# Where six layer-norm tiles are transposed inside the first cross-attention of a fused six-stage kernel

## The chip, the cores and the metric

The kernel runs on one core of a Trainium2 chip. A core has a matrix engine (TensorE, PE in the profile; its weight loads are PEld), a vector engine (DVE), a scalar engine (ACT), GpSimd (POOL), and a queue that issues transfers (SP). Each engine works through its own instructions in order, and waits on semaphores for the others. [...] The metric is the device time of one execution in microseconds. Three runs of the kernel before gave 1981.14, 1982.46 and 1980.77 us, a median of 1981.14 us.

## The reference

The whole is two layers of a Perceiver: cross-attention, a Mamba-like mixer, a routed feed-forward, a second cross-attention, causal self-attention, and a quantized feed-forward, each on the layer norm of a residual stream `x` of 16 x 64 tokens by 512. The change lies in the first cross-attention, and in the layer norm that the second step needs:

```python
def _layernorm(x, axis=-1, eps=1e-05):
    m = jnp.mean(x, axis=axis, keepdims=True)
    v = jnp.var(x, axis=axis, keepdims=True)
    return (x - m) / jnp.sqrt(v + eps)
...
    # first cross-attention: 16 heads of 32, 1601 context keys for each of 16 sequences
    qh = (q @ Wq + bq).reshape(B, LQ, HEADS, D_K).transpose(0, 2, 1, 3)
    kh = (k @ Wk + bk).reshape(B, LKV, HEADS, D_K).transpose(0, 2, 1, 3)
    vh = (v @ Wv + bv).reshape(B, LKV, HEADS, D_K).transpose(0, 2, 1, 3)
    scores = jnp.einsum('bhqd,bhkd->bhqk', qh, kh) * scale
    attn = jax.nn.softmax(scores, axis=-1)
    out = jnp.einsum('bhqk,bhkd->bhqd', attn, vh)
    concat = out.transpose(0, 2, 1, 3).reshape(B, LQ, D_MODEL)
    return concat @ Wo + bo
...
x = x + _L0_xattn_ref(_layernorm(x, axis=-1), ctx_512, ctx_512, ...)
x = x + _L0_attn_ref(_layernorm(x, axis=-1), ...)
```

## The kernel before

All is float32. The 1024 tokens are eight tiles ("groups", `g`) of 128 rows; a group holds two sequences of 64. The first cross-attention runs over 32 units `u` (a sequence and half of its heads: `u // 2` is the sequence) and a 33rd pass that finishes the last unit. Every instruction in this loop is pinned (`pin`) to the order in which the program writes it, on each engine, so there is no planner between the text and the queues. One pass of the loop holds work of three units at once:

- `next_k`: projections of the keys of unit `u`, eight of them (`k_proj`, line 221), each two pairs of matmuls into a PSUM tile of the pool `ps_mm`, which ACT copies out with the bias (line 231). `ps_mm` has two buffers, and the value projections and `project` use it too.
- `maxima(u - 1)` and `shift(u - 1)` (lines 323 and 331): four transposes, a reduction on DVE (line 329), four transposes that spread the maxima, and seven additions on DVE (line 342). Their PSUM tiles `mt` and `nb` share the pool `ps_mx`, tag `mx`, which has one buffer. `maxima` follows the first of the eight key projections, `shift` the second.
- `next_exps`: the exponentials of unit `u - 1` on ACT (line 350), between the later key projections and behind the first scores.
- `scores(u, 0)`, `scores(u, 1)`, `scores(u, 2)`: matmuls into two double banks `sc0` and `sc1`, emptied by ACT (`keep`, line 278) and compared by DVE (line 294). The third call has a rest of 65 keys, `scl`, of which one half goes into `ps_mx`.
- `attend(u - 1, 0)` behind `scores(u, 1)`, and `attend(u - 1, 1)` behind `scores(u, 2)`: matmuls of 32 columns, tile `av`.
- `project(g)` when a group's four units are done, at `u` = 5, 9, 13, 17, 21 and 25 for the groups 0 to 5: four more matmuls, the addition to `x`, and `ln_stats` on DVE.

As soon as a group's `x` is final, its layer norm can be made for the next step. `ln_scale` (line 119) takes the square root of the variances on ACT and the reciprocal on DVE. The square root is not in the table of functions that Exp uses, so the program loads a table ahead of it, and another ahead of the next Exp. `ln_norm` (line 123) scales a group on DVE, at the start of a pass. `ln_transpose` (line 130) transposes the 128 x 512 result in four matmuls into one PSUM tile, and ACT copies it into `xnT` (line 135). `xnT` is the same tensor as `qo`, the queries and outputs of the attention, whose columns of a finished group are free. `NORM0` says which pass makes which group. Behind `ln_norm`, POOL adds a bias row to the group's `x` for the next step (line 143); this is not pinned and goes to where its operand is ready.

The kernel before takes the square roots of the groups 0 to 3 in pass 17 and of 4 and 5 in pass 25, and norms the groups in the passes 18, 19, 20, 21, 27 and 28. In each of these, the transposes stand between the third and the fourth key projection (lines 518 to 521) and use a buffer of `ps_mm`.

Of the kernel before, what the change touches and what calls it, by code (L numbers as in the profile page):

```python
# [9 lines left out]
F32 = mybir.dt.float32  # L10
# [5 lines left out]
P = 128  # L16
# [11 lines left out]
LN_EPS = 1e-5  # L28
NEG = -1.0e30

NORM0 = {18: (0,), 19: (1,), 20: (2,), 21: (3,), 27: (4,), 28: (5,)}
NPREP = 30
RND = 12582912.0
QMAX = 32767.0
# [8 lines left out]
def nkeys(c):  # L43
    return min(P, LK - c * P)
# [3 lines left out]
def perceiver_kernel(ctx: ExitStack, tc: tile.TileContext, x_d, ctxT_d, ctx_d, cols_d, rows_d,  # L48
# [5 lines left out]
    def pool(stack, name, bufs=1, side="left", **kw):  # L54
        return stack.enter_context(
            tc.tile_pool(name=name, bufs=bufs, side=side, reuse_waits="tile", **kw))
# [44 lines left out]
    def row(at, n=D):  # L101
        return rows[:, at:at + n]
# [16 lines left out]
    def ln_scale(g0, g1, pin=free):  # L119
        pin(s.activation(rstd[:, g0:g1], mv[:, g0:g1, 1], AF.Sqrt, bias=eps))  # L120
        pin(v.reciprocal(rstd[:, g0:g1], rstd[:, g0:g1]))
# [5 lines left out]
                            ALU.subtract, ALU.mult))  # L127
        return xn

    def ln_transpose(g, xn, ps_pool, pin=free, dst=None):  # L130
        ps = ps_pool.tile([P, 4, P], F32, name="ps", tag="mm")
        for c in range(4):
            pin(pe.transpose(ps[:, c, :], xn[:, c * P:(c + 1) * P], ident))  # L133
        dst = xnT if dst is None else dst
        pin(s.copy(dst[:, :, g * P:(g + 1) * P], ps))
# [58 lines left out]
    with ExitStack() as st1:  # L194
# [18 lines left out]
        ps_mm = pool(st1, "ps_mm", bufs=2, space=PSUM)  # L213
        pin = tc.keep_in_program_order

        def pmm(out, lhsT, rhs, start=True, stop=True):
            pin(pe.matmul(out, lhsT=lhsT, rhs=rhs, start=start, stop=stop))  # L217
# [33 lines left out]
        def scores(u, g):  # L251

            ks = range(4 * g, 4 * g + 4)
            last = KC - 1
            if g == 0:
                sts[u] = stp.tile([P, KC, 512], F32, name="st", tag="st")
            st = sts[u]
            sc = [ps_sc.tile([P, 4, 2 * P], F32, name="sc", tag=f"sc{r}") for r in range(2)]  # L260

            def one_chunk(out, k):
                n = nkeys(k)
                for i in range(2):
                    for r in range(2):
                        rows_ = slice(64 * r, 64 * r + 64)
                        pmm(out[r][:n, i * P:(i + 1) * P],
                            kts[u, i][rows_, k * P:k * P + n], qds[u % 2][rows_, i, :])

            for k in ks:  # L270
                one_chunk([sc[r][:, k - ks[0], :] for r in range(2)], k)
            if last == ks[-1] + 1:
                tail = [ps_mx.tile([P, 2 * P], F32, name="scl", tag="mx"),
                        ps_mm.tile([P, 2 * P], F32, name="scl", tag="mm")]
                one_chunk(tail, last)

            def keep(r):
                pin(s.copy(st[:, ks[0]:ks[-1] + 1, r * 256:(r + 1) * 256], sc[r]))  # L278

            if g == 0:  # L280
                keep(0)
                keep(1)
                first[u] = sc
                return

            keep(1)
            if last == ks[-1] + 1:
                n = nkeys(last)
                for r in range(2):
                    pin(s.copy(st[:n, last, r * 256:(r + 1) * 256], tail[r][:n]))  # L290
            for r in range(2):
                rm = rms[u][:, :, r * 256:(r + 1) * 256]
                for z in (0, 2):
                    pin(v.tensor_tensor(rm, rm, sc[r][:, z:z + 2, :], ALU.max))  # L294
                if r == 0:
                    keep(0)
# [48 lines left out]
        def exps(u, k):  # L345

            n = min(2, KC - k)
            m = nkeys(k + n - 1)
            f = flat(u)
            pin(s.activation(f[:m, k:k + n, :], f[:m, k:k + n, :], AF.Exp))  # L350
            if u == 2 * B - 1:
                return
            if k == 2:
                accs[u] = mxp.tile([P, 2, 512], F32, name="acc", tag="acc")
                pin(gp.tensor_tensor(accs[u], f[:, 0:2, :], f[:, 2:4, :], ALU.add))  # L355
            elif 2 < k and n == 2:
                pin(gp.tensor_tensor(accs[u], accs[u], f[:, k:k + 2, :], ALU.add))  # L357
            elif n == 1:
                pin(gp.tensor_tensor(accs[u][:m, 0], accs[u][:m, 0], f[:m, k, :], ALU.add))
# [72 lines left out]
        with ExitStack() as stq:  # L432
# [8 lines left out]
            for h in range(2):  # L441
                for e in range(4):
                    ps = psq.tile([P, 512], F32, name="ps", tag="mm")
# [24 lines left out]
        ps_mx = pool(st1, "ps_mx", space=PSUM)  # L468

        for u in range(U + 1):  # L470
            old, new = u >= 1, u < U
            k_at = iter(range(0, KC, 2))

            def next_exps(n):
                for _ in range(n if old else 0):
                    exps(u - 1, next(k_at))

            def next_k(i, z):
                if old and new:
                    k_proj(u, i, z)  # L480

            def next_v(*ks):
                for k in ks:
                    v_proj(u, k)

            if 0 < u <= NPREP:
                piece_load(u - 1, prep)
            if new:
                diagonal(u)
            if u < G:  # L490
                pin(gp.tensor_tensor(x[:, u, :], x[:, u, :], row(R_BO0), ALU.add))

            normed = [(g, ln_norm(g, pin)) for g in NORM0.get(u, ())]
            next_k(0, 0)
            if old and new:
                maxima(u - 1)
            next_k(0, 1)
            if not new:


                project(G - 2, lambda: maxima(u - 1), lambda: shift(u - 1))
                divide(u - 2)
                for k in range(0, KC, 2):
                    exps(u - 1, k)
                    for z in range(k, min(k + 2, KC)):
                        attend_chunk(u - 1, z)
                b, hf = (u - 1) // 2, (u - 1) % 2
                rs = mxp.tile([P, 2, LQ], F32, name="rs", tag="rs")
                pin(v.reciprocal(rs, avs[u - 1][2]))
                for i in range(2):  # L510
                    pin(v.tensor_tensor(qo[:, 2 * hf + i, b * LQ:(b + 1) * LQ], avs[u - 1][i],
                                        rs[:, i], ALU.mult))
                break
            if old:
                shift(u - 1)
            if u >= 2:
                divide(u - 2)
            next_k(0, 2)
            for g, xn in normed:
                ln_transpose(g, xn, ps_mm, pin)  # L520
            next_k(0, 3)
            for z in range(4):
                next_k(1, z)
                next_exps((1, 1, 0, 2)[z])
            if 1 < u <= NPREP + 1:
                piece_turn(u - 2, room[:, u % 2, :], pin)
            next_v(0, 1)
            scores(u, 0)
            next_exps(3)
            next_v(2)  # L530
            first_max(u, 0)
            next_v(3)
            first_max(u, 1)
            next_v(4, 5)
            if 0 < u <= NPREP:
                piece_scale(u - 1, pin)
            g = (u - 2) // 4
            if u >= 2 and (u - 2) % 4 == 3 and g < G - 2:
                project(g)
                ln_stats(g, pin)  # L540
                if g in (3, 5):
                    ln_scale(0 if g == 3 else 4, g + 1, pin)
            scores(u, 1)
            if old:
                attend(u - 1, 0)
            next_v(6, 7, 8, 9)
            if old:
                acc = accs[u - 1]
                pin(v.tensor_tensor(acc[:, 0], acc[:, 0], acc[:, 1], ALU.add))
            if 0 < u <= NPREP:  # L550
                piece_steps(u - 1, pin)
            scores(u, 2)
            if old:
                attend(u - 1, 1)
                sum_up(u - 1, accs[u - 1][:, 0])
            if 0 < u <= NPREP:
                piece_round(u - 1, pin)
            next_v(10, 11)
            last_max(u)
            next_v(12)  # L560
            if u % 2 and u // 2 + 2 < B:
                load_ctx(u // 2 + 2)
# [28 lines left out]
    with ExitStack() as st2:  # L591
# [141 lines left out]
        mt, xn = None, None  # L733
        for g in range(G):
# [7 lines left out]
            if g >= 2:  # L742
                ln_scale(g - 2, g - 1, pin)
                xn = ln_norm(g - 2)
# [31 lines left out]
    with ExitStack() as st3:  # L776
# [132 lines left out]
        for q in range(2):  # L909
            t = slice(q * 512, (q + 1) * 512)  # L910
            for i in range(NBLK):
                ps = ps3.tile([P, 512], F32, name="ps", tag="mm")
# [65 lines left out]
    with ExitStack() as st4:  # L978
# [18 lines left out]
        ps_mm = pool(st4, "ps_mm4", bufs=3, space=PSUM)  # L997
# [120 lines left out]
    mx = const.tile([P, 5, 24], F32, name="mx", tag="mx")  # L1118
# [132 lines left out]
    with ExitStack() as st6:  # L1251
# [30 lines left out]
        with ExitStack() as sta:  # L1282
# [57 lines left out]
            for f in range(FC):  # L1340
# [5 lines left out]
                for h in range(2):  # L1346
                    t = slice(h * 512, (h + 1) * 512)
                    ps = ps6.tile([P, 512], F32, name="ps", tag="mm")
# [118 lines left out]
```

## Time and profile before

| | |
|---|---|
| three runs, median (us) | 1981.14 |
| the profiled execution, its own time (us) | 1979.56 |
| its span, from the first to the last instruction (us) | 1977.8 |
| granted TensorE clock | 0.993 |
| ACT line 120, square root | 20 times, 294 / 296 / 302 ns |
| ACT line 120, table loads ahead of it | 13 times, 1283 ns each |
| ACT line 135, copy of a transposed group into `xnT` | 40 times, 576 / 586 / 726 ns |
| DVE line 126, scaling of a group | 46 times, 513 / 544 / 723 ns |

The three figures are the least, the median and the most. A busy PE says that matmuls were in flight; since they overlap, the time of a group of matmuls is best read from the start of its first to the start of what follows. Windows of a pass, below, are cut at the start of the reduction on line 329, which occurs once in each pass from 1 to 32.

### The profile page before, as it was taken

How to read it: one execution, taken by the hardware profiler on the slowest of the kernel's cores; microseconds unless marked ns; L12 is line 12 of the kernel's file. 1: busy time of each engine (PE TensorE's matmuls, PEld its weight loads, DVE VectorE, ACT ScalarE, POOL GpSimd, SP SyncE). 2: the span in 40 equal slices, each digit the busy share in tenths (PEclk: the TensorE clock that was granted, in tenths of full speed). 3: DMA queues.
4: the chain of work that ended last, by engine and by line, in shares of the span. 5: the costliest groups of instructions: out<-in, count | busy, mean ns of one | idle time of the engine just before them, and what ended most of it. 6: DMA issues, size and time to landing. Idle time of an engine off the chain costs nothing.

```text
span 1977.8 us, 38953 instructions
## 1 busy us (share of the span) xinstructions
PE 1925.4 (97%) x17069; PEld 1214.5 (61%) x17069; DVE 1167.2 (59%) x1934; ACT 812.5 (41%) x1137; POOL 621.3 (31%) x464
## 2 busy tenths in 40 slices
PE   8999999999999999999999999999999999999599
PEld 4677777677777777777777754445444554444234
DVE  3577777777777777777777765722203334329651
ACT  2445454455545454454545556310202232316700
POOL 1245555454545445464554522211002000000100
PEclk9999999999999999999999999999999999999899
DMA  6012011111211110121110030530155981001001
GB/s 216 1 46 56 14 55 46 45 23 45 56 46 23 46 50 18 46 56 36 32 46 18 29 135 23 172 96 1 53 213 200 407 335 64 0 19 45 0 0 43
DMA packets 110075, 141.14 MB, mean 71 GB/s; under 512 B 79520, under 2 KB 82096, under 8 KB 106320
## 3 DMA queue, kind: packets, MB, share of 16 engines
q1 hardware_dynamic: 109904, 138.64, 21.0%
q8 instruction: 134, 2.20, 0.5%
q14 instruction: 37, 0.30, 0.0%
HBM read 127.02 MB, written 11.60 MB: 70 GB/s over the span
## 4 chain that ended last, share of the span: by engine, by line
PE 93%; DVE 2%; issue 2%; ACT 2%; DMA 1%; POOL 0%; POOLq 0%; SPq 0%; ACTq 0%; DVEq 0%
PE ps L217 39%; PE ps L59 24%; PE sc L217 12%; PE av L217 6%; PE po L59 4%; PE u L217 2%; PE ps L133 1%; PE pbc L59 1%; PE mt L327 1%; PE nb L336 1%; PE scl L217 1%; PE pd L59 1%; POOL gate L1344 0%; DVE st L342 0%; PE pg L59 0%
## 5 line engine op out<-in xcount | busy, mean ns | idle before, releaser
L217 PE MATMUL ps<-wkv,ctxT 128*128 128x256 f32 (+1 forms) x1664 | 393.6, 387 | 1.8 <-DVE vt L242 1.6
L217 PE MATMUL ps<-ctxT,wkv 128*128 128x400 f32 (+1 forms) x1024 | 365.2, 503 | 11.5 <-DMA ctxT<-in_ctxT_dram 7.3
L217 PEld LDWEIGHTS ps<-wkv,ctxT 128*128 128x128 f32 (+1 forms) x1664 | 295.5, 185 | 75.4 <-ACT kt L231 13.8
L278 ACT COPY st<-sc 128x1024 f32<-128x1024 f32 x192 | 191.9, 1016 | 294.2 <-PE sc L217 281.5
L357 POOL TENSOR_TENSOR acc<-acc,st 128x1024 f32<-128x1024 f32 x124 | 293.4, 2366 | 22.6 <-ACT st L350 17.5
L242 DVE TENSOR_TENSOR vt<-ps,rows 128x256 f32<-128x256 f32 (+1 forms) x416 | 174.8, 421 | 176.8 <-PE ps L217 176.7
L217 PEld LDWEIGHTS ps<-ctxT,wkv 128*128 128x128 f32 x1024 | 189.1, 190 | 140.4 <-ACT kt L231 10.1
L231 ACT ACTIVATE kt<-ps,cols 128x400 f32<-128x400 f32 (+1 forms) x256 | 152.3, 595 | 270.5 <-PE ps L217 270.5
L342 DVE TENSOR_TENSOR st<-st,nb 128x1024 f32<-128x1024 f32 (+1 forms) x224 | 239.0, 1138 | 34.5 <-PE nb L336 34.5
L350 ACT ACTIVATE st<-st 128x1024 f32<-128x1024 f32 (+1 forms) x224 | 212.1, 993 | 7.2 <-DVE st L342 6.9
L217 PEld LDWEIGHTS sc<-qd,kt 64*128 64x128 f32 x3072 | 178.9, 188 | 34.4 <-issue 24.4
L217 PE MATMUL sc<-qd,kt 64*128 64x128 f32 x3072 | 197.3, 278 | 0.0
L294 DVE TENSOR_TENSOR rm<-rm,sc 128x512 f32<-128x512 f32 x256 | 169.2, 681 | 40.0 <-PE sc L217 35.6
L355 POOL TENSOR_TENSOR acc<-st 128x1024 f32<-128x1024 f32 x31 | 73.2, 2362 | 319.3 <-issue 174.7
L59 PE MATMUL ps<-xnT,w 128*128 128x512 f32 x256 | 112.7, 594 | 0.0
L59 PE MATMUL ps<-w,hT 128*128 128x512 f32 x256 | 110.2, 592 | 0.0
L217 PE MATMUL av<-st,vt 128*32 128x64 f32 x6656 | 108.5, 220 | 0.9 <-ACT st L350 0.7
L217 PEld LDWEIGHTS av<-st,vt 128*32 128x32 f32 x6656 | 97.2, 110 | 11.8 <-issue 5.3
L180 POOL TENSOR_TENSOR w<-w,wsc 128x512 f32<-128x512 f32 x36 | 38.5, 1068 | 196.8 <-DVE w L179 196.8
L1344 POOL TENSOR_TENSOR gate<-up,gate 128x1024 f32<-128x1024 f32 x5 | 11.8, 2357 | 249.1 <-ACT up L1343 249.1
L59 PEld LDWEIGHTS ps<-w,hT 128*128 128x128 f32 x256 | 48.6, 190 | 61.2 <-issue 61.2
L59 PE MATMUL ps<-xnT,wuT 128*128 128x512 f32 x192 | 82.8, 592 | 0.0
(246 smaller groups left out, 2197.5 us busy)
## 6 DMA issues: line engine op xcount, KB each, us to landing
cT<-in_ctxT_dram SPq DMA_DIRECT2D x16, 1601.0 KB, 9.7
cN<-in_ctx_dram SPq DMA_DIRECT2D x16, 1536.0 KB, 11.0
ctxT<-in_ctxT_dram SPq DMA_DIRECT2D x15, 1601.0 KB, 6.4
mk<-kept SPq DMA_DIRECT2D x16, 512.0 KB, 3.9
w<-in_w_dram SPq DMA_DIRECT2D x1, 4096.0 KB, 13.4
w<-in_w_dram SPq DMA_DIRECT2D x4, 1024.0 KB, 7.3
w<-in_wgate_dram SPq DMA_DIRECT2D x12, 256.0 KB, 2.8
wgt<-room SPq DMA_DIRECT2D x48, 64.0 KB, 2.0
```

The lines of the kernel that those rows point to most:

```text
L59: pe.matmul(out, lhsT=lhsT, rhs=rhs, start=start, stop=stop)
L133: pin(pe.transpose(ps[:, c, :], xn[:, c * P:(c + 1) * P], ident))
L180: pin(gp.tensor_tensor(w, w, sc.unsqueeze(2).to_broadcast([P, 16, 32]), ALU.mult))
L217: pin(pe.matmul(out, lhsT=lhsT, rhs=rhs, start=start, stop=stop))
L231: pin(s.activation(kts[u, i][:, o:o + n], ps[:, :n], AF.Identity, bias=col(C_BK0 + c)))
L242: pin(v.tensor_tensor(t[:n, :], ps[:n, :], row(R_BV0 + e, 256)[:n, :], ALU.add))
L278: pin(s.copy(st[:, ks[0]:ks[-1] + 1, r * 256:(r + 1) * 256], sc[r]))
L294: pin(v.tensor_tensor(rm, rm, sc[r][:, z:z + 2, :], ALU.max))
L342: pin(v.tensor_tensor(f[:m, k:k + n, :], f[:m, k:k + n, :], nb[:m].unsqueeze(1).to_broadcast([m, n, 512]), ALU.add))
L350: pin(s.activation(f[:m, k:k + n, :], f[:m, k:k + n, :], AF.Exp))
L355: pin(gp.tensor_tensor(accs[u], f[:, 0:2, :], f[:, 2:4, :], ALU.add))
L357: pin(gp.tensor_tensor(accs[u], accs[u], f[:, k:k + 2, :], ALU.add))
```

## The change

Three edits. `ln_transpose` gets the tag of its PSUM tile as an argument. In the loop of the first attention, the call moves from between the third and the fourth key projection to behind `scores(u, 1)`, ahead of `attend(u - 1, 0)`, and takes its tile from `ps_mx` and not from `ps_mm`. And the six groups are normed in the passes 26 to 31, with one `ln_scale` for all six in pass 25; that of pass 17 is gone. `ln_norm` stays at the start of its pass.

```diff
-NORM0 = {18: (0,), 19: (1,), 20: (2,), 21: (3,), 27: (4,), 28: (5,)}
+NORM0 = {26: (0,), 27: (1,), 28: (2,), 29: (3,), 30: (4,), 31: (5,)}
...
-    def ln_transpose(g, xn, ps_pool, pin=free, dst=None):
-        ps = ps_pool.tile([P, 4, P], F32, name="ps", tag="mm")
+    def ln_transpose(g, xn, ps_pool, pin=free, dst=None, tag="mm"):
+        ps = ps_pool.tile([P, 4, P], F32, name="ps", tag=tag)
...
             next_k(0, 2)
-            for g, xn in normed:
-                ln_transpose(g, xn, ps_mm, pin)
             next_k(0, 3)
...
                 ln_stats(g, pin)
-                if g in (3, 5):
-                    ln_scale(0 if g == 3 else 4, g + 1, pin)
+                if g == 5:
+                    ln_scale(0, g + 1, pin)
             scores(u, 1)
+            for g, xn in normed:
+                ln_transpose(g, xn, ps_mx, pin, tag="mx")
             if old:
                 attend(u - 1, 0)
```

Built, the changed kernel has on ACT one square root and two table loads fewer in this stage, on DVE one reciprocal fewer, and the same number of instructions on POOL and SP. The order on ACT in a normed pass is: the two `keep` copies of `scores(u, 1)`, the copy of line 135, then the first `keep` of `scores(u, 2)`. On PE the transposes stand right between the scores and `attend`, and the first of them carries no semaphore wait of its own. The scaling on DVE and POOL's addition of line 143 move with their passes. Behind the first attention, the order on all engines is as before.

## The prediction

> **What bounds the kernel now.** I read the engine totals and the chain of waits first, on the page:
>
> ```profile
> PE 1925.4 (97%) x17069; PEld 1214.5 (61%) x17069; DVE 1167.2 (59%) x1934; ACT 812.5 (41%) x1137; POOL 621.3 (31%) x464
> PE 93%; DVE 2%; issue 2%; ACT 2%; DMA 1%; POOL 0%; POOLq 0%; SPq 0%; ACTq 0%; DVEq 0%
> ```
>
> TensorE sets the end: 93% of the chain is its own matmuls. So an edit counts by what it adds to or takes from PE's sequence, and work of DVE, ACT and POOL counts only where PE waits for it. To see where PE waits, I cut the first attention into its passes. The columns are the stretch, its length, then busy time and instructions of PE, PEld, DVE, ACT and POOL, the granted clock and the DMA share; here are passes 17, 18, 19, 23, 25, 26 and 27:
>
> ```profile
> 621.25:658.07 36.82, 36.82 (x421) 26.51 (x420) 27.52 (x47) 18.74 (x26) 16.96 (x12) 1.00 0.10 18
> 658.07:693.53 35.46, 34.30 (x417) 25.40 (x416) 25.89 (x42) 19.02 (x26) 18.26 (x13) 1.00 0.20 60
> 693.53:727.82 34.29, 34.04 (x417) 25.57 (x416) 25.90 (x43) 17.64 (x25) 18.25 (x13) 1.00 0.10 20
> 833.21:866.54 33.33, 33.33 (x413) 25.14 (x412) 25.33 (x41) 17.16 (x24) 16.98 (x12) 1.00 0.11 21
> 899.88:936.70 36.82, 36.82 (x421) 26.52 (x420) 27.07 (x46) 18.73 (x26) 16.95 (x12) 1.00 0.10 19
> 936.70:971.21 34.51, 33.60 (x413) 24.98 (x412) 25.90 (x43) 18.55 (x25) 16.99 (x12) 1.00 0.20 61
> 971.21:1005.50 34.29, 34.04 (x417) 25.56 (x416) 25.90 (x43) 17.63 (x25) 18.24 (x13) 1.00 0.11 20
> ```
>
> A plain pass (23) takes 33.33 us and PE is busy for all of it. A pass with a norm (19, 27) takes 34.29: 0.96 more, of which 0.25 is idle PE. Passes 17 and 25 hold a projection and a square root; both take 36.82, while pass 21, with a projection and a norm, took 37.77, which is 36.82 + 0.95: the square root itself costs its pass nothing. But the pass after it pays: pass 26 has no norm and takes 34.51, 1.18 too many, and pass 18 takes 35.46, which is 33.33 + 0.95 + 1.18. The timelines say why: PE in passes 20, 23 and 26, then ACT in 26 (start, length, engine, line, in brackets the idle time before and who ended it):
>
> ```profile
> 728.97 0.60 PE L336 MATMUL nb<-ident,nm 128*128 128x128 f32 x4
> 729.40 1.51 PE L217 MATMUL ps<-ctxT,wkv 128*128 128x400 f32 x4
> 730.75 0.60 PE L133 MATMUL ps<-ident,xn 128*128 128x128 f32 x4
> 731.60 6.99 PE L217 MATMUL ps<-ctxT,wkv 128*128 128x400 f32 x20 [0.25 <-ACT kt L231]
> ...
> 834.79 8.23 PE L217 MATMUL ps<-ctxT,wkv 128*128 128x400 f32 x24
> 842.86 1.98 PE L217 MATMUL ps<-wkv,ctxT 128*128 128x256 f32 x8
> ...
> 850.41 2.06 PE L217 MATMUL sc<-qd,kt 64*128 64x128 f32 x32
> 852.39 1.66 PE L217 MATMUL av<-st,vt 128*32 128x64 f32 x104
> ...
> 946.08 1.61 PE L217 MATMUL ps<-ctxT,wkv 128*128 128x400 f32 x4 [0.91 <-ACT kt L231]
> ```
>
> ```profile
> 943.19 1.28 ACT L350 ACT_TABLE_LOAD   x1
> 944.48 1.06 ACT L350 ACTIVATE st<-st 128x1024 f32<-128x1024 f32 x1
> 945.45 0.58 ACT L231 ACTIVATE kt<-ps,cols 128x400 f32<-128x400 f32 x1
> ```
>
> In the normed pass the transposes hold one of `ps_mm`'s two buffers, so the next key projection waits for ACT to empty the other. In pass 26 ACT loads Exp's table back between two copies of keys, and PE waits for the second.
>
> **The square root of pass 17 goes.** On PE it costs nothing in its pass; the table load behind it costs pass 18 the same 1.18 us as that of pass 25 costs pass 26 (35.46 - 34.29 = 1.17; 34.51 - 33.33 = 1.18). One of the two disappears: -1.18. The one that stays, with six columns in place of two, is no dearer: the forms of four and of two columns lie within 294 to 302 ns.
>
> [...]
>
> **The transposes leave the key projections.** From the end of `shift`'s transposes to the first value projection, the plain pass needs 842.86 - 834.79 = 8.07; pass 20 needs 738.42 - 729.40 = 9.02 (its value projection starts at 738.42). So each leaving brings -0.95: 0.43 for four transposes in a row (as `nb`'s, 728.97 to 729.40), 0.42 of waiting for the buffer until 731.60, and 0.10 further on, since 20 matmuls then take 6.82 where they take 8.07 - 1.35 = 6.72. The gap closes altogether, as plain passes show with no waits at all. Six times: -5.72.
>
> **They arrive behind the second scores.** Here the trace has no such pair of neighbours, so I bound it. From below: a row of four transposes between matmuls of the same shape takes 0.43. From above: what they cost now, 0.95. The place lies between 64-row scores and 32-column attention. A group of one shape runs 0.16 to 0.17 over into the next of the same shape (728.97 + 0.60 against 729.40); where the shape changes it is only 0.08 (850.41 + 2.06 against 852.39). One change of shape is there already, from `sc` to `av`; the transposes make two of it. So I take 0.43 + 0.09 to 0.10 = 0.53, nearest to the rows of both neighbours: six times, +3.18.
>
> [...]
>
> The waits there: the transposes need `xn`, scaled at the start of the pass, and the bank of `nb`, whose last reader on DVE (line 342) ends in pass 23 at 842.5, ten before 852.39. The copy (line 135, 0.58) stands on ACT behind the second `keep`, 853.94 + 1.01 = 854.95, and ends by 855.5; ACT's next work starts at 859.76, and the rest of the scores, which wants the bank, at 859.52 before the shift and 860.05 behind it. That is 4.5 us of cover; if it were gone, every microsecond over it would stop PE. Behind that wait stand the second half of `attend` and the last value projections.
>
> **What else moves.** `ln_norm` (0.53 to 0.54) stays ahead of the reduction of line 329, which waits for PE's transposes anyway (DVE idles 12.6 us there over 26 passes, 0.48 each); in pass 20 it ended at 727.80 and the reduction began at 727.82. If that cover went, 0.5 us would reach `shift`. POOL's addition of line 143 (1.26) moves to passes in which POOL otherwise idles 8.5 us ahead of its sums. The lost reciprocal (0.12 to 0.20) was hidden. No transfer is moved or passed in SP's queue; `xnT` is complete in pass 31, while the next stage begins after pass 32.
>
> **The sum.** -1.18 - 5.72 + 3.18 = -3.72. Span 1977.8 becomes 1974.1, the profiled time 1979.56 becomes 1975.84. The profiled execution lies 1.58 under the median of the runs; on the median it is 1981.14 - 3.72 = **1977.4 us**, that is -0.19%. With both ends of the one open price (0.43 and 0.95) the sum runs from -4.3 to -1.2.
>
> **Rivals.** (a) *The second change of shape is free.* The array may empty while the transposes' weights are loaded; each group then costs 0.43, the sum is -1.18 - 5.72 + 2.58 = -4.32, and the time 1976.8. For it: PEld is only 61% busy. Against: every change of shape between neighbours in a pass has the short overlap.
> (b) *The whole switch of tables counts*, the load to the square root, the root and the load back, 1.28 + 0.30 + 1.28 = 2.86 in place of 1.18: the sum is -5.40, the time 1975.7. For it: all three stand in ACT's order ahead of work that PE waits for. Against: pass 17 is as long as pass 21 less its norm. [...]
> (c) *The wait goes along*: the transposes find a new one of the old size, each costs 0.95 again and only the square root is won: 1981.14 - 1.18 = 1980.0. Against it: the bank has been free for ten microseconds.
> (d) *Slower: the single bank of `ps_mx` becomes a lock.* If the copy slips behind the first `keep` of the third scores, it starts when that ends (859.76 + 0.53 + 1.01 = 861.3), is done at 861.88, and `scl` waits 1.83 from 860.05 on. Six times 1.83 = 11.0, less 3.72: 1988.4. It decides from the point at which the copy is over 4.5 us late, and is a loss from 5.1. Against it: ACT idles 4.81 between the `keep`s, and the built order has the copy ahead.
>
> **How the numbers follow.** What a measurement can tell from no change is 0.2%, here 3.96 us: the line lies at 1977.18, a hair under the forecast. Forecast 0.60, of which the scatter of the runs (1980.77 to 1982.46) puts 0.28 below the line and 0.32 above; (a) 0.27, 0.25 of it below; (b) 0.02 below; (c) 0.05 within; (d) 0.06, of which 0.05 slower and 0.01, a lock that eats just the gain, within. Faster 0.28 + 0.25 + 0.02 = 0.55; same 0.32 + 0.02 + 0.05 + 0.01 = 0.40; slower 0.05. The range reaches from (b), 1975.7, rounded down to 1975.6, to 1979.6, which is the forecast plus the 1.7 between the least and the most of the runs and 0.5 for a `shift` that comes later in some passes; (c) and (d), 0.11, stay outside.
>
> **What would show it.** Passes 18 to 20 take 33.33, 21 takes 36.82, 26 takes 33.33 + 1.18 + 0.53 = 35.04, 27 to 30 take 33.86 each. From the first transpose of line 133 to `av`: 0.53; 0.43 would be (a), 0.95 (c). Line 120 has 12 table loads. Of PE's waits for line 231, the six of 0.25 are gone, and one of 0.91 is left of two. It is wrong if `scl` waits for line 135, if the plain passes are no longer 33.33, or if time changes behind the first attention.

## The result, and the profile after

Over 22 runs each, taken in turn, the changed kernel has a median of 1977.27 us (1976.36 to 1979.58) and the kernel before 1980.07 us (1979.45 to 1982.5). The ratio is 0.9985, with a 95% interval from 0.998 to 0.9991: a gain of 0.15%, clear of no change, but within the 0.2% that the prediction set as its line. The forecast of 1977.4 us lies 0.1 us off. That it lies so close is luck, since two errors nearly cancel. With 22 runs the median of the kernel before came out 1.07 us lower than with the three runs that the forecast started from, and the gain between the medians is 2.80 us, 0.92 less than the 3.72 forecast. Besides, the 22 runs of the changed kernel fall into three groups, 11 at 1976.36 to 1976.85, 7 at 1977.69 to 1978.06 and 4 at 1979.21 to 1979.58: the median lies in the middle of a gap in which there is no run.

The engine totals and the chain of waits of the changed kernel look as before; TensorE still sets the end:

```profile
PE 1925.8 (97%) x17069; PEld 1216.4 (62%) x17069; DVE 1166.8 (59%) x1933; ACT 809.1 (41%) x1134; POOL 621.3 (31%) x464
PE 94%; DVE 2%; issue 2%; ACT 1%; DMA 1%; POOL 0%; SPq 0%; ACTq 0%; POOLq 0%; DVEq 0%
```

ACT has lost 3.4 us, 2.86 of them one root and two table loads (0.30 + 2 x 1.28), and DVE one reciprocal. The passes show the rest. Here are 17, 18, 25, 26 and 27 of the changed kernel, cut as in the prediction, with the same columns:

```profile
621.40:658.22 36.82, 36.82 (x421) 26.60 (x420) 27.03 (x45) 17.14 (x24) 16.95 (x12) 1.00 0.10 19
658.22:691.55 33.33, 33.33 (x413) 25.17 (x412) 25.34 (x41) 17.14 (x24) 17.00 (x12) 1.00 0.21 63
895.04:931.85 36.81, 36.81 (x421) 26.52 (x420) 27.52 (x46) 19.00 (x26) 16.93 (x12) 1.00 0.09 19
931.85:966.95 35.10, 34.19 (x417) 25.43 (x416) 25.97 (x42) 19.03 (x26) 18.25 (x13) 1.00 0.19 60
966.95:1000.87 33.92, 33.92 (x417) 25.59 (x416) 25.85 (x43) 17.63 (x25) 18.24 (x13) 1.00 0.11 21
```

Pass 18 is plain now. A pass with a norm (27) takes 33.92, 0.59 over a plain one, and PE is busy for all of it; the 0.25 of idle PE is gone. Pass 26 has both the norm and the load of Exp's table: 33.33 + 1.18 + 0.59 = 35.10. The timelines of PE and of ACT in pass 26 of the changed kernel show both places:

```profile
933.43 6.89 PE L217 MATMUL ps<-ctxT,wkv 128*128 128x400 f32 x20
941.23 1.61 PE L217 MATMUL ps<-ctxT,wkv 128*128 128x400 f32 x4 [0.91 <-ACT kt L231]
...
950.23 2.06 PE L217 MATMUL sc<-qd,kt 64*128 64x128 f32 x32
952.21 0.66 PE L133 MATMUL ps<-ident,xn 128*128 128x128 f32 x4
952.80 1.66 PE L217 MATMUL av<-st,vt 128*32 128x64 f32 x104
...
959.93 0.28 PE L217 MATMUL scl<-qd,kt 64*65 64x128 f32 x2
```

```profile
938.35 1.28 ACT L350 ACT_TABLE_LOAD   x1
939.64 1.06 ACT L350 ACTIVATE st<-st 128x1024 f32<-128x1024 f32 x1
...
953.76 1.01 ACT L278 COPY st<-sc 128x1024 f32<-128x1024 f32 x1 [0.39 <-DVE rm L294]
954.67 0.59 ACT L135 COPY xnT<-ps 128x512 f32<-128x512 f32 x1
960.17 1.02 ACT L278 COPY st<-sc 128x1024 f32<-128x1024 f32 x1 [4.91 <-PE sc L217]
```

From the first transpose (952.21) to the attention (952.80), 0.59 us pass. The copy ends at 955.26, and `scl`, which wants the bank, starts at 959.93 without a wait. Of PE's waits within the first attention (in all, times, longest), those for the copies of keys read as follows, first in the kernel before, then in the changed kernel:

```profile
PE ps L217 <- ACT kt L231: 4.2, 9, 0.9
PE ps L217 <- ACT kt L231: 1.8, 2, 0.9
```

The six of 0.25 and the one behind the root of pass 17 are gone. Of the two that are left, one is the 0.91 above; the other, 0.85 in pass 1, is in both kernels and also stands behind a load of Exp's table.

From the reduction of line 329 in pass 1 to that in pass 32, the kernel before needs 1063.28 us and the changed kernel 1059.90: a gain of 3.38 us. That is more than the 2.80 between the medians, and in the two profiled executions only 1.50 was left (1979.56 and 1978.06). The 1.88 us between are, but for 0.01 us of rounding, 1.39 lost behind the first attention, 0.35 outside the span (the execution's time less its span) and 0.15 ahead of pass 1. So two questions go to the experiments: whether root and place are worth what the prediction says, and where the rest is given back.

### The profile page after: what moved, and what is told of

It is laid out like the page before. It is cut to its first block, busy times and chain, and to the rows that moved or that the text cites. A ratio compares the mean times of both kernels' runs of the same rounds, so it can differ in the third digit from the quotient of the medians.

```text
span 1976.0 us, 38949 instructions
## 1 busy us (share of the span) xinstructions
PE 1925.8 (97%) x17069; PEld 1216.4 (62%) x17069; DVE 1166.8 (59%) x1933; ACT 809.1 (41%) x1134; POOL 621.3 (31%) x464
## 4 chain that ended last, share of the span: by engine, by line
PE 94%; DVE 2%; issue 2%; ACT 1%; DMA 1%; POOL 0%; SPq 0%; ACTq 0%; POOLq 0%; DVEq 0%
PE ps L217 39%; PE ps L59 24%; PE sc L217 12%; PE av L217 6%; PE po L59 4%; PE u L217 2%; PE ps L133 1%; PE pbc L59 1%; PE mt L327 1%; PE nb L336 1%; PE scl L217 1%; PE pd L59 1%; POOL gate L1344 0%; PE busy L217 0%; DVE st L342 0%
## 6 DMA issues: line engine op xcount, KB each, us to landing
w<-in_w_dram SPq DMA_DIRECT2D x1, 4096.0 KB, 13.4
```

## The experiments

The length of the first attention, below, is always that of the 31 passes just named. It comes from one trace for each kernel. That is enough for it: plain passes agree within 0.01 us between all traces, and the three traces whose first attention is that of the changed kernel (two of them differ from it only behind it) give 1059.88 to 1059.91 us.

**One root, old place.** From the changed kernel, the transposes go back:

```diff
             next_k(0, 2)
+            for g, xn in normed:
+                ln_transpose(g, xn, ps_mm, pin)
             next_k(0, 3)
...
             scores(u, 1)
-            for g, xn in normed:
-                ln_transpose(g, xn, ps_mx, pin, tag="mx")
```

> The transposes go back between the third and the fourth key projection and into ps_mm; the passes 26 to 31 and the single square root of the changed kernel stay. Theory (root and place are two gains that add): pass 18 takes 33.33 us, pass 26 33.33 + 1.18 + 0.95 = 35.46, the passes 27 to 30 34.29 each; the first attention ends 1.18 us earlier than in the kernel before and 2.2 later than in the changed kernel. Rival (what helps is that the norms stand in later passes, wherever in the pass): passes 27 to 30 take 33.92 as in the changed kernel.

Measured: pass 18 33.33, pass 26 35.47, passes 27 to 30 34.29 each; 1062.08 us in all, 1.20 less than in the kernel before. Here are passes 26 and 27:

```profile
931.73:967.20 35.47, 34.31 (x417) 25.40 (x416) 25.89 (x43) 19.02 (x26) 18.23 (x13) 1.00 0.19 59
967.20:1001.49 34.29, 34.04 (x417) 25.56 (x416) 25.89 (x43) 17.62 (x25) 18.25 (x13) 1.00 0.11 20
```

The later passes win nothing by themselves; the rival falls.

**New place, old passes and roots.** `NORM0` and the condition of `ln_scale` are those of the kernel before.

```diff
-NORM0 = {26: (0,), 27: (1,), 28: (2,), 29: (3,), 30: (4,), 31: (5,)}
+NORM0 = {18: (0,), 19: (1,), 20: (2,), 21: (3,), 27: (4,), 28: (5,)}
...
-                if g == 5:
-                    ln_scale(0, g + 1, pin)
+                if g in (3, 5):
+                    ln_scale(0 if g == 3 else 4, g + 1, pin)
```

> The old passes (18 to 21, 27, 28) and both square roots, with the transposes behind the second scores in ps_mx. Theory: pass 18 takes 33.33 + 1.18 + 0.59 = 35.10 us, 19 and 20 33.92, 26 34.51 (a root behind it, no norm), 27 and 28 33.92; the first attention ends 6 x (0.95 - 0.59) = 2.2 us earlier than in the kernel before and 1.18 later than in the changed kernel. Rival (the place pays only with the later passes): 19 and 20 stay at 34.29.

Measured: pass 18 35.10, 19 and 20 33.92, 26 34.51, 27 and 28 33.92; 1061.08 us, 2.20 less than in the kernel before. Here are passes 18 and 19:

```profile
658.03:693.13 35.10, 34.19 (x417) 25.40 (x416) 25.97 (x42) 19.03 (x26) 18.24 (x13) 1.00 0.19 59
693.13:727.05 33.92, 33.92 (x417) 25.57 (x416) 25.84 (x42) 17.64 (x25) 18.24 (x13) 1.00 0.10 21
```

1.20 + 2.20 = 3.40 against the 3.38 of both together: the two parts add up and don't touch each other.

**New place, the other bank.**

```diff
-                ln_transpose(g, xn, ps_mx, pin, tag="mx")
+                ln_transpose(g, xn, ps_mm, pin)
```

> The changed kernel with the transposes in the new place, but in a buffer of ps_mm. Theory (the bank matters, because ps_mm has two buffers and the value projections behind the attention want both): the copy on ACT ends some 2.5 us behind the first transpose, the second value projection wants the buffer 0.44 us before that, so TensorE waits 0.4 to 0.5 once and the passes 27 to 30 take 34.3 to 34.4 us. Rival (only the place matters): 33.92 as in the changed kernel, with no wait of TensorE.

Measured: passes 27 to 30 take 33.97 to 33.98, 0.06 more than in the changed kernel, and no 0.4. My expectation misses by a size, and the rival by 0.06: I took a value projection for two matmuls of 0.22 us. The program writes two, but the trace has 16 matmuls for four projections, four for each, so the second projection wants the buffer 0.43 later than I reckoned, at just about the time when the copy is done. At the new place either bank would do; that it is `ps_mx` is worth 0.06 us a group.

**Old place, the new bank.** As in the first experiment, but with `ps_mx` and `tag="mx"`.

> The transposes go back between the third and the fourth key projection, but stay in the bank of ps_mx. Theory (place and bank belong together: at the old place the bank is still read by the seven additions of line 342): the transposes wait for the last addition, some 6.3 us behind the third key projection, and the passes 27 to 30 take about 40 us, the whole some 35 to 40 us more than the changed kernel. Rival (the waits at the old place were for ps_mm alone, so a bank of its own ends them): the passes take 33.8 to 34.0.

Measured: 2030.35 us, passes 27 to 30 42.1 to 43.2 us; the first attention takes 53.6 us more than in the changed kernel, where 35 to 40 were expected. The timeline of PE in this kernel shows the wait, in its place and its length:

```profile
977.51 0.60 PE L336 MATMUL nb<-ident,nm 128*128 128x128 f32 x4
977.95 1.51 PE L217 MATMUL ps<-ctxT,wkv 128*128 128x400 f32 x4
985.77 1.09 PE L133 MATMUL ps<-ident,xn 128*128 128x128 f32 x4 [6.31 <-DVE st L342]
```

PE waits 6.31 us until line 342 has read the bank. The 2 to 3 us a pass beyond the expected 40 are the clock, which the expectation left out: the four transposes take 1.09 here and not 0.60, and the trace grants half the clock for 6.8 to 10.2 us around the end of each of these waits; the mean granted clock of this execution is 0.981, that of the kernel before 0.993. In pass 27 the half clock lasts 5.95 us past the wait; half of that, 3.0, is about what the pass takes beyond 40. The single bank is a lock at the old place and none at the new one.

**Each transpose twice.** This tells which part of the 0.59 us repeats with each transpose and which comes once for the group.

```diff
         for c in range(4):
-            pin(pe.transpose(ps[:, c, :], xn[:, c * P:(c + 1) * P], ident))
+            for _ in range(2 if tag == "mx" else 1):
+                pin(pe.transpose(ps[:, c, :], xn[:, c * P:(c + 1) * P], ident))
```

> Each of the six groups is transposed twice in its new place, the second time over the first, one after the other for each column block. Theory (0.59 us of a group are four steps of 0.109, which repeat, and 0.15 for the two changes of shape, which do not): the four more cost 0.44 and the passes 27 to 30 take 34.36 us. Rival (0.15 is a cost of each transpose): they take 33.92 + 0.59 = 34.50.

Measured: passes 27 to 30 take 34.36, 0.44 more for four more transposes. The 0.15 over 4 x 0.109 comes once for the group.

**One place earlier, among the value projections.**

```diff
+            for g, xn in normed:
+                ln_transpose(g, xn, ps_mx, pin, tag="mx")
             scores(u, 1)
-            for g, xn in normed:
-                ln_transpose(g, xn, ps_mx, pin, tag="mx")
```

> The changed kernel with the transposes one place earlier, between the value projections and the second scores, where the shape changes anyway. Theory (0.15 of the 0.59 us of a group are two changes of the matmul's shape): a group costs 0.44, the passes 27 to 30 take 33.77 us, pass 26 34.95, and the first attention ends 0.9 us earlier than in the changed kernel. Rival (the 0.15 comes with each group of transposes): 33.92 as in the changed kernel.

Measured: pass 26 34.95, passes 27 to 30 33.77, in all 1059.00 us, 0.90 less than the changed kernel. PE's timeline in this kernel:

```profile
981.67 2.32 PE L217 MATMUL ps<-wkv,ctxT 128*128 128x256 f32 x10
983.83 0.60 PE L133 MATMUL ps<-ident,xn 128*128 128x128 f32 x4
984.36 2.06 PE L217 MATMUL sc<-qd,kt 64*128 64x128 f32 x32
```

The group lies next to full-sized matmuls on one side, the change of shape to `sc` is there in any case, and the 0.15 is gone. So it belongs to the second change of shape.

**Exp's table loaded early.**

```diff
             scores(u, 1)
+            if u == 25:
+                warm = small.tile([P, 1], F32, name="warm", tag="warm", bufs=1)
+                pin(s.activation(warm, eps, AF.Exp))
```

> The changed kernel with one exponential of a 128x1 tile on ACT behind the second scores of pass 25, whose result nobody reads: Exp's table is loaded there, where ACT idles 4.8 us, and not between two copies of keys in pass 26. Theory (1.18 us of a square root is TensorE's wait for the table that is loaded back): pass 26 takes 33.92 us in place of 35.10, pass 25 stays at 36.82. Rival (the load costs what it costs, wherever it stands): pass 25 takes 38.0 and nothing is won.

Measured: pass 25 36.82, pass 26 33.92; 1058.71 us, 1.19 less than the changed kernel, so the rival falls. ACT's timeline in this kernel has the load in a gap of ACT in pass 25:

```profile
919.34 1.01 ACT L278 COPY st<-sc 128x1024 f32<-128x1024 f32 x1 [0.47 <-DVE rm L294]
920.37 1.28 ACT L544 ACT_TABLE_LOAD   x1
921.66 0.20 ACT L544 ACTIVATE warm<-eps 128x1 f32<-128x1 f32 x1
925.08 1.01 ACT L278 COPY st<-sc 128x1024 f32<-128x1024 f32 x1 [3.21 <-PE sc L217]
```

So the price of a square root was the place of the load behind it. The load takes 1.28 here too, and the next instruction starts where it ends, at 921.66.

**The stalls ahead of the last step, filled.** Behind the first attention the profiled execution of the changed kernel took 839.58 us to the end of its span, that of the kernel before 838.19. PE stalls twice there, for 2.11 and 1.07 us, in both kernels; here in the changed one:

```profile
1683.35 1.09 PE L133 MATMUL ps<-ident,xn 128*128 128x128 f32 x8 [2.11 <-DVE mv L117]
1685.51 1.97 PE L133 MATMUL ps<-ident,xn 128*128 128x128 f32 x8 [1.07 <-DVE xn L126]
```

The traces differ there in the granted clock (the third number from the end). The half clock lasts 3.41 us in the kernel before and 6.83 in the changed kernel, and the lines are cut at its ends and into windows of 3.41 us; first the kernel before, then the changed kernel:

```profile
1685.11:1688.52 3.41, 1.09 (x9) 0.85 (x9) 3.41 (x10) 1.37 (x3) 0.00 (x0) 1.00 0.00 0
1688.52:1691.94 3.42, 3.42 (x11) 2.51 (x12) 2.71 (x8) 1.17 (x2) 0.00 (x0) 0.50 0.00 0
1691.94:1695.00 3.06, 3.06 (x8) 1.25 (x7) 2.90 (x8) 2.82 (x5) 0.00 (x0) 1.00 0.00 0
```

```profile
1681.01:1684.42 3.41, 1.30 (x9) 0.84 (x8) 3.34 (x11) 1.21 (x4) 0.00 (x0) 1.00 0.01 2
1684.42:1687.83 3.41, 2.34 (x11) 2.06 (x11) 2.83 (x6) 1.57 (x4) 0.00 (x0) 0.50 0.00 0
1687.83:1691.25 3.42, 3.42 (x5) 1.35 (x5) 3.29 (x10) 2.40 (x5) 0.00 (x0) 0.50 0.00 0
1691.25:1694.00 2.75, 2.75 (x7) 1.22 (x7) 0.58 (x2) 2.75 (x5) 0.00 (x0) 1.00 0.00 0
```

In both, a window in which PE was busy for little of the time (1.09 and 1.30 us) is followed by one at half clock. In the kernel before, PE is busy all through that one, and the full clock comes back behind it. In the changed kernel the second stall falls into it; with 2.34 us of busy PE a second window at half clock follows. So I filled the stalls with matmuls whose results nobody reads, which is what `busy` issues:

```diff
-            for g in range(4, G):
-                norm6(g, ps6)
...
+            busy(2, ident, x[:, G - 2, :])
+            for g in range(4, 6):
+                norm6(g, ps6)
+            busy(1, ident, x[:, G - 1, :])
+            for g in range(6, G):
+                norm6(g, ps6)
```

> The changed kernel with matmuls whose results nobody reads in the two stalls of TensorE ahead of the last step (four passes over 512 columns ahead of the transposes of groups 4 and 5, two ahead of those of 6 and 7). Theory (the runs fall into groups some 1.3 us apart because those stalls bring one or two windows of 3.4 us at half clock, depending on where the stalls fall in the windows): no half clock is granted between 1680 and 1695 us, the time from the reduction of pass 32 to the end falls from 838.0 to 839.6 us to 836.5 to 837.5, and the runs lie closer together. Rival (the groups come from somewhere else, the start of the program or transfers): the runs lie in the same three groups, and the part behind the first attention takes 838 or more.

Measured: 1976.71 us, 11 runs within 0.68 us (1976.51 to 1977.19) where the 22 of the changed kernel spread over 3.2. The clock there, in the stretches ahead of the last step of this kernel:

```profile
1672.00:1682.00 10.00, 10.00 (x37) 5.35 (x36) 8.18 (x17) 3.07 (x6) 0.00 (x0) 1.00 0.00 1
1682.00:1692.00 10.00, 8.35 (x31) 3.82 (x30) 8.99 (x23) 5.58 (x11) 0.00 (x0) 1.00 0.00 0
```

No half clock is granted in them, as expected. But the part behind the first attention takes 838.25, not 836.5 to 837.5: a single window at half clock costs nothing that can be seen against none. The kernel before (838.19) and that with the new place and old passes (838.00) had one, and the kernel with the early table had none and took 838.29. Only a second one costs, 839.58 in the changed kernel and 838.9 to 839.7 in the five others here that had two (one root, other bank, twice, among the values, two calls).

**Both kernels filled, side by side.** The same edit on the kernel before, and the filled changed kernel once more.

> The kernel before, with the same unread matmuls in the two stalls ahead of the last step as in the run that filled them in the changed kernel. Theory (the half-clock windows there, and not the first attention, scatter the runs of both kernels): the runs lie within 1 us, near the least of the kernel before, 1979.6 to 1980.2, and the filled changed kernel stands 3.2 to 3.4 us below, the size that the passes show. Rival (the change itself is worth only the 2.8 us between the medians): the two filled kernels lie 2.6 to 2.9 apart.

> The filled changed kernel once more, on the same chip and beside the same runs as the filled kernel before. Theory: 1976.5 to 1976.9, 3.2 to 3.4 us below the other.

Measured: 1979.82 us (1979.51 to 1981.29) and 1977.04 us (1976.44 to 1978.52), 2.78 apart; the least of each are 3.07 apart. Of the expectation only the median of the filled kernel before holds. The runs still scatter over 1.8 to 2.1 us, the second with the very kernel that had kept within 0.68 above, and the medians are as far apart as the rival said (2.6 to 2.9), and not 3.2. In the profiled execution of the filled kernel before, some 1.5 us were lost at the start, where half the clock was granted from 13.4 to 16.8 us (its span is 1979.6, the shortest of the same kernel's runs 1977.8): the reduction of pass 1 starts at 77.98, in all other traces at 76.3 to 76.6. So the stalls ahead of the last step are not the only source of scatter. That they are one rests on the traces: the profiled execution of the changed kernel, with two windows, is of the middle group of its runs (1978.06), that of the kernel before, with one, of the least (1979.56). The narrower spread of the filled kernels (0.68 and 2.1 us against 3.2, 1.8 against 3.1) says the same less surely, with half as many runs. No trace of the changed kernel is of its slowest group.

**Two calls for the roots.** What remains between 3.38 and some 3.0 lies outside the span. In each of the runs, execution time less span was 1.66 to 1.79 us in the kernels with the old roots (before, new place with old passes, before filled) and 2.04 to 2.15 in all that have the new one: 0.35 more. One edit tells whether an instruction more does that:

```diff
-                    ln_scale(0, g + 1, pin)
+                    ln_scale(0, 4, pin)
+                    ln_scale(4, g + 1, pin)
```

> The changed kernel with the square roots of pass 25 in two calls, one behind the other (groups 0 to 3, then 4 and 5): one square root and one reciprocal more, so that DVE has as many instructions as in the kernel before, and no more table loads. The time of an execution lies 1.66 to 1.79 us over its span in the kernels with the old square roots and 2.04 to 2.15 in those with the new one. If that follows the count of instructions on DVE, it is 1.7 here; if it follows the table loads or the passes, 2.1. The passes stay as in the changed kernel (35.10 and 33.92 us).

Measured: 1976.93 us on a span of 1975.2, a difference of 1.73; the passes stay at 35.10 and 33.92. With one root and one reciprocal more, the 0.35 us are back outside the span. The kernel with the early table has one instruction more on ACT alone, and 2.12. So it goes with the number of roots and reciprocals (DVE has 1934 instructions on the one set of pages, 1933 on the other), which this edit can't tell apart, and neither with table loads nor with passes. What the 0.35 us are is open: the traces don't reach outside the span.

**All that gained.** The transposes among the value projections, the early table, the filled stalls.

> All three parts that gained: the transposes between the value projections and the second scores, Exp's table loaded back in pass 25, and the stalls ahead of the last step filled. Theory: the parts add up, the first attention ends 0.9 + 1.18 = 2.1 us earlier than in the changed kernel, and the runs lie at 1974.4 to 1974.9, 5.3 us below the filled kernel before. Rival (the copy on ACT, now ahead of the second scores' copies, and the early table load get into each other's way or into that of the copies): pass 26 takes over 34.0 us.

Measured: 1974.78 us (1974.24 to 1975.96), a ratio to the kernel before of 0.9973 (0.9962 to 0.9984); passes 26 to 30 take 33.77 each, so the rival falls, and the first attention 1057.79. The median is 5.04 us under the filled kernel before, where 5.3 were expected; in the passes it is 5.47, and the 0.35 outside the span explains most of the rest. It is the fastest of the kernels here.

## Why the prediction was right

- *The root*: -1.18 expected, -1.20 measured alone. The early load takes 1.19 off with the root left in its place, so the cost was the wait for Exp's table.
- *The leaving of the key projections*: as expected, passes 18 to 20 are plain and the waits of 0.25 are gone. The prediction counted two waits of 0.91 where the list has three: it left out that of pass 1, which the change doesn't touch.
- *The arrival*: the mis-sized term. 0.53 a group was expected, 0.59 measured, which makes 0.35 us for six groups. The change of shape was priced by the overlap of neighbours (0.10). It costs 0.15, since the second transpose also comes late: in pass 27 the four start at 986.130, 986.294, 986.403 and 986.512, so the first step is 0.164 and the others are 0.109, while among the values all three are 0.109 to 0.110. Rival (a), no price for the second change of shape, is out; its size, 0.44, is real, but one place earlier.
- *The waits*: the copy ended 4.7 us ahead of `scl`, where 4.5 of cover were expected; rivals (c) and (d) did not occur. At the old place a lock of (d)'s kind is real, at 6.31 us a pass.
- *The whole switch of tables*, rival (b): out. Pass 17 takes 36.82 with the root and its load and 36.82 without them, and pass 18 at 33.33 has won the 1.18 and no more.
- *The sum*: in the passes -3.38 for -3.72. The prediction then carried it to the median unchanged, and that is the step that failed: 0.35 us came back outside the span, which leaves 3.0, about the distance of the least runs (3.1), and the medians of runs that scatter in groups gave 2.80.
- *The signs of being wrong*: one of the three came true. The part behind the first attention took 839.58 us in place of 838.19, while the prediction let no time change there. The order of instructions there is the same; what differs between the two profiled executions is the second window at half clock. Whether the change makes such a window more frequent is not shown.
- *The chances*: 0.55 stood on more than 0.2%, 0.40 on the case that came. What tipped it were the 0.27 for rival (a), against which the prediction itself had the stronger rows.

## What to carry to other kernels

Where one engine is busy without a gap, a step is worth what its neighbours make of it: the same four transposes cost 0.95 us where they take a buffer that the next step wants, 0.59 between two other shapes of matmul, and 0.44 beside matmuls of their own shape. The square root on ACT, which needs another table than Exp, cost its 1.18 us where the load back stands, not where the root stands; an unread Exp in a gap of ACT moved the load there. And a free buffer is one at a place, not one by name: the bank that cost nothing behind the scores stopped TensorE for 6.3 us ahead of them.

## What the runs showed of the hardware

- In the profiled execution of the kernel before, the granted clock was 0.50 from 1688.52 to 1691.94 us and from 1862.61 to 1886.50, in that of the changed kernel from 1684.42 to 1691.25, from 1861.91 to 1885.81 and in the last 1.4 us. The stretches that ended within the span were thus 3.41, 6.83 and twice 23.89 us long; the two long ones began while PE waited 22.4 us for `gate`. In the 3.41 us ahead of the short ones PE was busy for 1.09 and 1.30 us. The half clock went on behind 3.41 us with 2.34 us of busy PE, and each of the four stretches ended behind 3.41 us in which PE was busy throughout. At which share of busy PE it comes and goes was not shown.
- Where these stretches fall against the work differs between the two executions: the first of them starts 2.16 us behind the end of the 2.11 us stall in the kernel before (1688.52 against 1686.36), and 1.07 us behind it in the changed kernel (1684.42 against 1683.35). A second window at half clock in the stalls ahead of the last step cost 0.7 to 1.5 us: the part behind the first attention took 838.9 to 839.7 us, against 838.19.
- The part of an execution's time that lies outside its span was 1.66 to 1.79 us in the four kernels with 1934 instructions on DVE and 2.04 to 2.15 in the nine with 1933, in every run. One root and one reciprocal make the difference, and I can't say why.
